# Applying a Fourier layer's score modes: elementwise on three engines instead of two-diagonal matrix products

## The chip, the cores and the metric

One Trainium2 chip, one of its cores. A core has five engines with queues of their own: TensorE (PE in the profile; its weight loads are PEld), VectorE (DVE), ScalarE (ACT), GpSimd (POOL) and SyncE (SP, which here issues most of the DMAs). Each engine works through its queue in order and waits on semaphores for the others. Matrix products read SBUF and write PSUM; DVE and ACT read both memories, and POOL works on SBUF here. All arithmetic is float32. The metric is the device time of one execution in microseconds (us), and lower is better.

## What is computed

Two layers of the same kind, each `x = x + layer(groupnorm(x))`, on `x` of shape (2 images, 56 channels K, 128, 128). Inside a layer stands an attention over the 56 channels whose keys, queries and values are Fourier layers with 8 heads A. Cut to what matters here (the layer's text in the reference is longer; `b` image, `i` input, `o` output):

```python
def spectral_conv(x, w, b):
    xf = jnp.fft.rfft2(x, norm='forward')
    top = jnp.einsum('bihw,iohw->bohw', xf[:, :, :M1, :M2], _c(w[0]))
    bot = jnp.einsum('bihw,iohw->bohw', xf[:, :, -M1:, :M2], _c(w[1]))
    of = jnp.zeros((B, Co, H, W // 2 + 1), dtype=xf.dtype)
    of = of.at[:, :, :M1, :M2].set(top).at[:, :, -M1:, :M2].set(bot)
    y = jnp.fft.irfft2(of, s=(H, W), norm='forward')
    return y + b[None, :, None, None]
...
('K', 1, A), ('Q', 1, A), ('V', 1, A), ('P', A, 1), ('M0', 1, 1), ('M1', 1, 1)
```

With M1 = M2 = 16 only 32 x 16 complex modes of each channel take part. The score of channels k and l in head a is a sum over space of query times key; by Parseval's rule it is a sum over the modes of `conj(X_k) * u_a * X_l`, where the complex number `u_a`, one for each mode and head, is made of the weights of K and Q. What the spectral part doesn't hold comes from the Gram matrix of the channels. This complex number times mode is the work that the change moves.

## The kernel before

**Work and order.** The program is first written as a list of *units* (class `Work`): one call, or several that stay together, each with the engines that may do it: T (PE), V (DVE), S (ACT), G (POOL), Q (the SP queue). `ORDER`, a string, then gives every unit once with the letter of the engine that does it, in the order in which it is issued: each number is the step from the unit named before. A small `v` is DVE too, and makes the next POOL unit wait for the end of that one (`issue`). `PLACES` gives for every PSUM buffer that is taken the bank where it lies. Both strings are the result of a search. `AWAKE` lists 40 products on constants that the order puts between the others; they only keep TensorE's clock up.

**Stages of a layer**, for each image b: the plane is turned and normalised (`turned`, `modes_chain`), and its modes are made. `xf` (128 x 448) holds them: eight blocks t of 56 channels; the 128 partitions are two halves e, each with real parts in the first 32 rows and imaginary parts in the next 32. `gram` and `gram_chain` make the channels' Gram matrix with 256 products; then come `scores`, `values`, `softmax_chain`, `mix_chain`, `heads` and `norms_chain`, then the GELU stage and two more Fourier layers. The two images run interleaved, so that one image's scores stand beside the other's Gram products.

**The numbers.** `prepare` makes each layer's constants. `product` multiplies the weights of K and Q into `u_a`; `place` splits a complex number into parts with masks for the real and imaginary rows, the columns 3 and 4 of the constant `raw`; `relay` turns them by products on TensorE into the layout of the modes, into `tcs` (128 x 8 x 36: 16 columns for the scores, 16 for the values, 4 for the M0 and M1 layers). `build(WUv, tcs, 0)` spreads the 16 score columns into WU, 128 x 4096: for each block t and head a, and in each half, a 64 x 64 matrix whose only non-zero entries lie on two diagonals, real to real and real to imaginary. `build(WTv, tcs, 16)` does the same for the values, in WT.

**`scores`** runs over pairs of blocks t. For each pair, 32 small products (8 heads, 2 blocks, 2 halves; 64 x 64 by 64 x 56) put `u_a * X` into two PSUM banks, one copy by ACT or DVE brings them (128 x 896) into the room `UX`, of which there are two, and `scored` adds `xf` times `UX` to the score bank `sc` with 4 products. After four pairs two more products add the Gram matrix's part, and `softmax_chain` starts on DVE. So that four quadrants of the array can work at once, odd blocks come out with their halves exchanged; for them `modes_chain` keeps `xs`, a copy of the odd blocks with exchanged halves (two copies from PSUM of 64 x 224).

WU's room is used again later: `FB[b]`, 1792 columns for each image, takes the modes of the GELU stage and the rows of `h_chain`.

Of the kernel before, what the change touches and what calls it, by code (L numbers as in the profile page):

```python
# [11 lines left out]
ALU = mybir.AluOpType  # L12
# [9 lines left out]
0V 1Q 1S 1S 1Q 1S 1S 1V 1G 1V 1G 1V 1G 1V 1G 1Q 1S 1Q 1S 1Q 1S 1Q 1S 1Q 1S 37T 10G -12T 56G -77T 31Q 17Q -53T  # L22
72Q -60T -18T 17T 28V 20Q 6Q 3Q -73T 11T 26Q -23T 6T 65V -16Q 69G -136T 17T -11T 4T 1T 80T -17Q -1Q 15T -86T 90S
-20Q 21V -4S 1V -53Q 57T 1S 1V -33Q 34T 1S 1V -98T 99T 1S 1V 1T -87T 22Q 44G 22S 1V 1T 2V -72Q -29T 62Q 40T 2V
74V -181T 106S -40Q -57T -8T -6T -4T 191T 1V -80S -26G 370Q -392Q 386Q 7Q -264G 2v 3G -4V -193T 49Q 88T 1S -83Q
145T 1V -142Q 139V -145Q 146V -4T 8T 270Q -269V -134Q 132T 4T -159Q 158T 4T -13S 11V -73T 74T -152Q 1Q 164T -4S
-153Q 146V 1T -157Q 85V 79S 1S -7T 1S 10T 1T 1T 1T 1T -165Q 160S -2S -75G -93Q 92G 2G 1G 1G 1G 1V 1v 77T -76T 7G
57S -136Q -12Q 161T 1T 2S -72V 1V 1V 7T -15V 77V -162Q 66S 21V 7V -10V 11v -33T 102T -168Q 63T 106S -63V 77G
-187Q -11Q 120V -41S -81Q 107V 2T 293Q -392Q 64T 50V 63V -62V 63G -104S 26V -33T 112v -104V -7S 1V -11T -28V 48V
38T 2T 1V -60S 98V -97V 61V -1V -48V 84V 24T -115S 42G 86T -85G 88T -2S 219Q -304G -116Q 188S -64S 10G -66T 1S  # L30
1V 151T -148V 195V -64S -87G 12V 73T 4T 1S 15S -17T 4T 60T -134G 135V 1G -141T 142V 3v 119Q -184S 193Q -195T 9T
-6T 1T 207Q -196G 53S -57T 55S -143S 142v -49V 56T 117Q -404Q 39Q 101G 82T 68T -63V 61V -4G 5T -57S 1V 1T 59T
-2V 1T 4T -91V 89V 1T 10T 1T 1T 1T -112V 113T -103v 91V 1T -63S 1T -13S 79S -205G 42G 81T 1S 78V 11T -273Q 200V
3T 92G 70Q -159T 1T -19S 20T 1T 65T -25V -188V 187G 514v -498V -158G 104S 156Q -162V 71T -60T -10T 72S 19T -287V
757V 1V -607V 3V 113V 2T 490V -451T 452V 5v -480G 3S -86v 69V -14T -54T 67S -63V 1T 101S 457G -561S 53S 44T 1S
-31G 1S -64V -156G 157G 96T 1S -83G -10V 1T 1V -5V 73G -67G 73T 1S -17T 15T 3T -74V 1v 1T 34G -102G 141T 1S -90V
18V 53V -54v 75T 1S -70T 1V -36T 103T 3T 1T 11V -32G -180v 95S 118V 1S -87T 1V -70G 157v -13T 1S 3T -92T 1S 150Q
4T 1V 38Q -3Q -21Q -77S 99Q -90T 47T 1V -47S 8T 64Q 18Q -250G -2G 233Q -70T 1V 52T 15T -60T 1T 1T 435G -538V
151S 1S -218v 610G -382V -108G 50S 62Q -1Q 2T 1V -69T -2T 1V 49S 1S 21T 5S 1S 12Q 1Q -83v 65S 1S 18Q -5T 2Q -1V
5T 1V -135G 50T -328V 329V 85T -82V 95Q -97S 9V -8T 2T 1V 15V 76Q -150G 153Q -53T 58Q 146Q -239T 1V -6G 7G -6V  # L40
7V 86T 5Q -8Q 4V 2Q -88v 71S 1S 351G -332T -4Q 5V 141Q 3Q -26Q 2Q -180S -439T 482S 1S -103T 1S 27T 2V -1v 25T 1S
65T 5S 1S -5S -86T 1V 24T 21T 75G 89Q -163S -51v -68G 159S 118Q -207T 1V -14T 221T -220S 223Q 2Q 190G -193Q -5Q
4V 26Q -2Q -189T 1S 169T 1V 13Q -200V 22T 1V 16T 1S 148T 5S 1S 14Q 175G -340T 1V 145S 201G -6G 7G -188T 1V -159T
1V 177Q -17Q 22Q -3Q -16T 1V 38Q -58S 55Q -183T 1V 3T 1S 144T 5S 1S -149T 317G 7T -323V 326V -165Q -329G 495V
-3V 1V -165Q -38T 1S 39Q -7Q 2T -4Q 5V 26Q -41S -142T 8V 135S -142T 181Q -179S 159T 1V -161S 2T 2S -173G 292T 1S
38T -157V 3V 117T -115V -7S 4T 2T 2T 156S -41V -114V 2V 132T 17S 14T 2Q -11S 14Q -18S 11Q -343G 351T -36S -5T
-129G 2V 159Q 4V -162G 1V 1T 125S 5T 21T 1S 14V 1T 1S -166V 129V -130v 7T 1V 163S 1S -705T 538T 1V 300T 1S 1G 4T
4V -3V 1V 1V -313T 7T -6S -533T 540V 1G 8V 149S -121T 1V 98T 171T -170S 5T -132G 2Q -6T 302S -261V 1G 95V -125T
10V -9V -12S 1S 155T 1S -108T 103T 1S -94V -9V -4T -14G 126T 1V -99G 4Q 104V -8T 1T -114S 1S 114S -154T 155S
-150V 3Q 20Q 26Q -53S 1S -503V 795T -138T -142v 145V -130T -580T 709S 4V 2V -134S -20T 1S 150T 2T -132S 134T -8V  # L50
9V 2V -125G 2Q 122G 2V -112T 113G -112S -59Q 178G 118V -283S 47S -608T 845V -277T 1S -576T 1139Q -412V 1T 2V
-126T 1S -28S 29S 123V 7T 1V -728T 722T 1S 122V 9v -129T 1V -741T 587Q -10Q 293T -862T 863V 1G 6G -19V -856T
555Q 315V 3S 1S -133T 131S -873T 752V -753T 754G -204Q 194V 1G 381Q -364T 1V -186Q 195V 28T 10V 1G -53Q 102T 1S
# [23 lines left out]
2T 3V 2T 1T 29V 47Q -14Q 1Q -67S 5T 1V 1G 57Q 11Q -67V 1V 28Q -5Q -33S 43T 1V 4Q -37G 74T -24Q -49v 1T 3T 1S 92S  # L77
-46Q 21S -9Q 5Q -20Q -11V 3Q -22Q 90S -84Q 85G -76Q 73S 1G -73Q 40T -39Q -33V 93S -92v 4T 1V 17Q -16T 89G -12S
1G -49Q 58G -55Q -2Q 36T -52Q -13V 100T 4V 2S -32S 1G 30Q -4V 1Q -36T 1T 4V 2S 30S -31Q 17T 4V -25S 2S -1Q 9T 4V
8V 2S -13V 5S -4Q 11Q -10S 2Q 12S -1Q  # L80
"""

PLACES = [int(c) for c in (
# [1189 lines left out]
```

## Time and profile before

| | us |
|---|---|
| runs shown | 404.88, 405.82, 1596.27 |
| median of the runs | 405.82 |
| the profiled execution | 403.93 |
| its span in the trace | 402.1 |

One of the three runs, 1596.27, stands far from the others. The profile is of one execution; its mean granted clock is 0.958 of TensorE's full speed. Its page has the busy time of each engine, the span in 40 slices, the chain of work that ended last, and the costliest groups of instructions. Every record here has line 225, that of `issue`, as its source, so groups are told apart by the names of the tiles: `psum<-xf,WU` are the products with the two-diagonal matrices, `P<-psum 128x896` copies of a pair (and of turned planes), `WU<-tc,C` the builds. A product in float32 is recorded as two. In the rows by stretch the columns are: stretch, its length, the busy time of PE, PEld, DVE, ACT and POOL with the number of instructions, the granted clock, the share of the DMA engines, GB/s.

### The profile page before, as it was taken

To read this page: it belongs to the slowest core of one execution; us is meant where nothing else is said; L and a number is where in the kernel's file an instruction comes from. 1 tells how busy PE (TensorE), PEld (TensorE's weight loads), DVE (VectorE), ACT (ScalarE), POOL (GpSimd) and SP (SyncE) were. 2 spreads that over 40 slices of the span, in tenths; PEclk is the share of its full clock that TensorE was granted. 3 is DMA by queue.
4 is the path that set the end of the run, shared out by engine and by line. 5 is a ranking of instruction groups with operands and counts; after the bars stand their busy time and mean duration, and the time that the engine had idled before them with its cause. 6 is when DMAs were issued, how large, how long until landed. Compare 5 with 4: busy or idle time off the path is not lost.

```text
span 402.1 us, 16509 instructions
## 1 busy us (share of the span) xinstructions
PE 364.4 (91%) x7316; PEld 258.3 (64%) x7316; DVE 310.5 (77%) x576; ACT 229.9 (57%) x335; POOL 198.7 (49%) x199
## 2 busy tenths in 40 slices
PE   8879999999989999898899999999999799889960
PEld 5545985897665556567676885797675555557440
DVE  7886798586867987899878858496969966997861
ACT  1425675236448768556958767134469637994520
POOL 9638293426775393158319261122422670268390
PEclk9999999999998999899969999999999789999895
DMA  7878305000044334000401363520053413212766
GB/s 211 216 213 201 79 3 163 3 3 4 20 146 115 93 109 125 13 3 26 136 5 36 110 200 103 173 64 4 13 156 101 139 53 112 91 35 85 223 188 209
DMA packets 21324, 40.04 MB, mean 100 GB/s; under 512 B 4613, under 2 KB 5381, under 8 KB 21253
## 3 DMA queue, kind: packets, MB, share of 16 engines
q1 hardware_dynamic: 20002, 35.25, 30.2%
q10 hardware_dynamic: 1250, 3.74, 3.1%
q8 instruction: 57, 0.93, 1.0%
q14 instruction: 15, 0.11, 0.1%
HBM read 24.29 MB, written 14.68 MB: 97 GB/s over the span
## 4 chain that ended last, share of the span: by engine, by line
PE 56%; DVE 21%; ACT 8%; issue 5%; POOL 4%; DMA 3%; SPq 1%; POOLq 1%; DVEq 0%; ACTq 0%
PE psum L225 56%; DVE X L225 6%; DVE P L225 6%; ACT P L225 5%; POOL P L225 3%; DMA xr<-x 3%; DVE WU L225 2%; DVE stats L225 2%; ACT psum L225 2%; DVE WT L225 1%; SPq L225 1%; ACT WT L225 1%; DVE f L225 1%; POOLq L1267 1%; POOL rs L225 1%
## 5 line engine op out<-in xcount | busy, mean ns | idle before, releaser
L225 ACT COPY P<-psum 128x896 f32<-128x896 f32 (+5 forms) x56 | 45.4, 835 | 53.8 <-PE psum L225 31.1
L225 POOL TENSOR_TENSOR X<-X,gvr 128x1024 f32<-128x1024 f32 x22 | 51.7, 2363 | 22.6 <-DVE P L225 8.2
L225 PE MATMUL psum<-P 128*64 128x56 f32 (+2 forms) x1632 | 59.3, 228 | 0.0
L225 PEld LDWEIGHTS psum<-C,P 32*128 32x128 f32 (+4 forms) x1124 | 44.3, 169 | 22.0 <-issue 6.5
L225 PEld LDWEIGHTS psum<-P 128*64 128x64 f32 (+1 forms) x1632 | 53.1, 138 | 6.7 <-issue 3.4
L225 PE MATMUL psum<-C,P 32*128 32x128 f32 (+4 forms) x1124 | 53.3, 264 | 3.0 <-DVE X L225 1.3
L225 DVE SCALAR_TENSOR_TENSOR X<-psum,cols,xr 128x1024 f32<-128x1024 f32 x32 | 40.3, 1275 | 12.7 <-PE psum L225 7.5
L225 ACT ACTIVATE P<-psum,cols 128x1024 f32<-128x1024 f32 x32 | 35.1, 1110 | 13.0 <-PE psum L225 12.2
L225 POOL TENSOR_TENSOR P<-P,X 128x1024 f32<-128x1024 f32 x13 | 30.4, 2361 | 15.4 <-ACT P L225 12.3
L225 ACT COPY WT<-psum 128x896 f32<-128x896 f32 x28 | 25.1, 903 | 19.3 <-PE psum L225 18.2
L225 PE MATMUL psum<-X,BTx 57*64 57x512 f32 x256 | 35.1, 630 | 1.1 <-ACT psum L225 0.7
L225 DVE STREAM_TRANSPOSE P<-psum 128x448 f32<-128x448 f32 (+1 forms) x24 | 29.1, 1226 | 7.2 <-PE psum L225 7.0
L225 POOL TENSOR_TENSOR X<-P,X 128x1024 f32<-128x1024 f32 x11 | 26.8, 2459 | 14.1 <-DVE WT L225 8.2
L225 ACT ACTIVATE psum<-P 128x1024 f32<-128x1024 f32 x32 | 32.9, 1030 | 0.7
L225 PE MATMUL psum<-P,C 128*64 128x112 f32 (+2 forms) x296 | 30.4, 389 | 2.2 <-ACT WT L225 1.0
L225 PE MATMUL psum<-ones 128*128 128x256 f32 (+1 forms) x80 | 30.9, 519 | 1.1 <-DVE ones L225 1.1
L225 ACT ACTIVATE P<-P,sh,gv 128x1792 f32<-128x1792 f32 x12 | 21.9, 1876 | 10.6 <-DVE sh L225 6.8
L225 PEld LDWEIGHTS psum<-C,X 56*128 56x128 f32 x512 | 18.5, 138 | 9.5 <-issue 4.8
L225 PEld LDWEIGHTS psum<-P,C 128*64 128x64 f32 (+2 forms) x296 | 15.1, 142 | 14.3 <-DVE P L225 5.5
L225 PE MATMUL psum<-C,X 56*128 56x56 f32 x512 | 22.1, 227 | 1.7 <-DMA X<-x 1.1
L225 PE MATMUL psum<-C,WT 32*128 32x128 f32 (+1 forms) x544 | 21.0, 279 | 2.8 <-DVE P L225 1.4
L225 PEld LDWEIGHTS psum<-C,WT 32*128 32x128 f32 (+1 forms) x544 | 18.0, 184 | 6.8 <-issue 2.8
(224 smaller groups left out, 693.5 us busy)
## 6 DMA issues: line engine op xcount, KB each, us to landing
xr<-x SPq DMA_DIRECT2D x64, 112.0 KB
store<-X SPq DMA_DIRECT2D x64, 112.0 KB
xr<-store SPq DMA_DIRECT2D x64, 112.0 KB
X<-x SPq DMA_DIRECT2D x34, 112.0 KB
out<-P SPq DMA_DIRECT2D x32, 112.0 KB
out<-P SPq DMA_DIRECT2D x8, 224.0 KB
out<-P ACTq DMA_DIRECT2D x8, 224.0 KB
stage<-weights SPq DMA_DIRECT2D x4, 272.0 KB
```

The lines of the kernel that those rows point to most:

```text
L225: done = getattr(engines[letter.upper()], method)(*args, **kw)
L1267: with tile.TileContext(nc) as tc:
```

## The change

The number times the mode is made elementwise. With `u = p + iq`, the product's real row is `p*re - q*im` and its imaginary row `p*im + q*re`: the mode times one column, plus its partner row (real for imaginary and the reverse) times another, whose sign is put into the constant `raw`. So `place` isn't needed for the scores, `WU` is no longer built, and odd and even blocks have one form. For each pair of blocks, ACT multiplies `xf` by the first column, head by head and block by block: 16 instructions of 128 x 56 in one unit, into `UX`. DVE or POOL multiplies the partners `xs` by the second column (one operation of 128 x 896) into `FB[b]`, and DVE or POOL adds the two. `xs` is now the whole of `xf` with exchanged groups of 32 partitions: four copies of 32 x 448 that POOL, ACT or DVE may make, in one buffer that both images use. `relay` puts the score columns into `uc`, one buffer for each layer. WU's room shrinks to what `FB` needs.

`ORDER` and `PLACES` are new throughout: 1,528 units for 1,518, and so are the letters. Of the 32 new products and sums 16 are DVE's and 16 POOL's; of the 16 `xs` copies ACT makes 8, DVE 5 and POOL 3. Of ACT's copies of 896 columns 13 are left of 28, and some other units change engines (four scalings of X go from DVE to POOL, two scalings of planes from ACT to DVE). `AWAKE` is unchanged. Ahead of the last score product of their stage stood 1, 2, 2 and 1 of the four units of value products; now 1, 4, 4 and 3.

```diff
-        [own, mirror, -mirror, count * dc * N * re, count * dc * N * im, dc * re, dc * im], 1
+        [own, mirror, -mirror, count * dc * N, count * dc * N * (im - re), dc * re, dc * im], 1
...
-    WU, WT, WM = hold("WU", [N, 4096]), hold("WT", [N, 4096]), hold("WM", [N, 1024])
-    WUv, WTv = (t.rearrange("p (t a m) -> p t a m", t=8, a=HEADS) for t in (WU, WT))
+    WU, WT, WM = hold("WU", [N, 3584]), hold("WT", [N, 4096]), hold("WM", [N, 1024])
+    WTv = WT.rearrange("p (t a m) -> p t a m", t=8, a=HEADS)
...
+    XS, UX = [hold("xs", [N, 448])] * B, [P[b][:, 5344:7136] for b in range(B)]
...
-            place(t64, cpt[:, o : o + 16].rearrange("p (a c) t -> p a c t", c=2), re, im, k)
+            to = cpt[:, o : o + 16].rearrange("p (a c) t -> p a c t", c=2)
+            if k == 3:
+
+                for c, t in enumerate((re, im)):
+                    tt(who, to[:, :, c], t, _bc(rawc[:, k + c], 1, 8), ALU.mult)
+            else:
+                place(t64, to, re, im, k)
...
-        tcs = hold("tc", [N, 8, 36])
+        tcs, uc = hold("tc", [N, 8, 20]), hold(f"uc{layer}", [N, 8, 16])
...
-        build(WUv, tcs, 0)
-        relay(cpt, tcs, stage[:, :1024], 16, 16)
-        relay(cpt, tcs, stage[:, :1024], 32, 4)
-        build(WTv, tcs, 16)
+        relay(cpt, tcs[:, :, :16], stage[:, :1024], 16, 16)
+        relay(cpt, tcs[:, :, 16:], stage[:, :1024], 32, 4)
+        build(WTv, tcs, 0)
...
-        xs = P[b][:, 7840:8072]
-        clear("GV", xs[:, 224:], 0.0)
-        for e in range(2):
-            q, o = slice(64 * e, 64 * e + 64), slice(64 - 64 * e, 128 - 64 * e)
-            copy(
-                "SV", xs[o, :224].rearrange("p (u k) -> p u k", k=K),
-                px[q, :448].rearrange("p (u v k) -> p u v k", v=2, k=K)[:, :, 1, :],
-            )
+
+        xs = XS[b]
+        for q in range(0, N, 32):
+            copy("GSV", xs[q : q + 32], xf[q ^ 32 : (q ^ 32) + 32, :448])
...
-        def scored(t):
-            u = R["UX"][t // 2 % 2]
+        uc, xs = prs[L][2].rearrange("p t (a c) -> p c t a", c=2), grid(st["xs"])
+        for t in range(0, 8, 2):
+            flat = [r[:, 896 * (t // 2 % 2) : 896 * (t // 2 % 2) + 896] for r in (UX[b], FB[b])]
+            both = [z.rearrange("p (t a k) -> p t a k", t=2, a=HEADS) for z in flat]
+            with work.unit():
+                for k in range(2):
+                    for a in range(HEADS):
+                        S.activation(both[0][:, k, a], xv[:, t + k], AF.Copy, scale=uc[:, 0, t + k, a : a + 1])
+            tt("GV", both[1], _bc(uc[:, 1, t : t + 2], 3, K), _bc(xs[:, t : t + 2, :], 2, HEADS), ALU.mult)
+            tt("GV", flat[0], *flat, ALU.add)
             with work.unit():
                 for k in range(2):
                     score(
-                        (xf[:, K * t : K * t + 64], st["xs"][:, K * t // 2 : K * t // 2 + 64])[k],
-                        grid(u[:, 448 * k : 448 * k + 448]), start=(t + k == 0), stop=False,
+                        xf[:, K * t + K * k : K * t + K * k + 64], grid(flat[0][:, 448 * k : 448 * k + 448]),
+                        start=(t + k == 0), stop=False,
                     )
-
-        for t in range(0, 8, 2):
-            p = pair()
-            with work.unit():
-                for a in range(HEADS):
-                    for k in range(2):
-                        for e in range(2):
-                            o = e ^ k
-                            T.matmul(
-                                p[64 * o : 64 * o + 64, k, K * a : K * a + K], lhsT=WUv[64 * e : 64 * e + 64, t + k, a, :],
-                                rhs=xv[64 * e : 64 * e + 64, t + k, :], start=True, stop=True,
-                                tile_position=(64 * e, 64 * o), skip_group_check=True,
-                            )
-            copy("SV", R["UX"][t // 2 % 2].rearrange("p (k m) -> p k m", k=2), p[:, :, :448])
-            scored(t)
```

More of the change, by code (lines that the diff above doesn't have):

```diff
@@ L27 @@
[L27 to L41, printed above, removed]
```

129 lines of the change are left out of this document (72 added, 57 removed).

## The prediction

> **What bounds the kernel now.** I read the page first: busy times, then the chain that ended last.
>
> ```profile
> span 402.1 us, 16509 instructions
> PE 364.4 (91%) x7316; PEld 258.3 (64%) x7316; DVE 310.5 (77%) x576; ACT 229.9 (57%) x335; POOL 198.7 (49%) x199
> PE 56%; DVE 21%; ACT 8%; issue 5%; POOL 4%; DMA 3%; SPq 1%; POOLq 1%; DVEq 0%; ACTq 0%
> ```
>
> TensorE (PE) is busy for 91% of the span and carries 56% of the chain; ScalarE (ACT) is busy for 57%. That is an average. The change works in four stages, one for each layer and image: from the copy that makes the modes `xf` to the first softmax operation, which reads the finished scores. The timeline gives their ends; here are the start of the first stage and the ends of the first and the last.
>
> ```profile
> 40.48 0.51 ACT L225 COPY xf<-psum 128x448 f32<-128x448 f32 x1
> 65.00 0.40 DVE L225 TENSOR_TENSOR psum<-psum,rr 128x224 f32<-128x224 f32 x1 [0.47 <-PE psum L225]
> 282.31 0.38 DVE L225 TENSOR_TENSOR psum<-psum,rr 128x224 f32<-128x224 f32 x1
> ```
>
> The view of busy time by stretches, asked for these four, and then for the tile WU alone over stretches that hold the products which leave (last row):
>
> ```profile
> 40.50:65.00 24.50, 24.44 (x699) 20.72 (x699) 19.86 (x61) 16.65 (x23) 14.27 (x13) 1.00 0.24 57
> 78.30:103.30 25.00, 24.86 (x675) 20.86 (x674) 19.57 (x57) 10.55 (x16) 11.66 (x19) 1.00 0.02 4
> 225.50:247.70 22.20, 21.91 (x623) 18.09 (x622) 14.67 (x29) 16.51 (x29) 11.09 (x8) 1.00 0.47 144
> 263.20:282.30 19.10, 18.88 (x560) 15.87 (x561) 15.26 (x42) 6.00 (x11) 4.67 (x6) 1.00 0.05 14
> sum 90.80, PE 90.10 PEld 75.53 DVE 69.36 ACT 49.71 POOL 41.68; mean PE 22.52 PEld 18.88 DVE 17.34 ACT 12.43 POOL 10.42
> sum 71.00, PE 18.27 PEld 16.59 DVE 1.22 ACT 0.00 POOL 8.80; mean PE 4.57 PEld 4.15 DVE 0.30 ACT 0.00 POOL 2.20
> ```
>
> The columns are stretch, length, PE, weight loads, DVE, ACT, POOL, then the granted clock. In the four stages PE is busy for 90.10 of 90.80 us, so they are PE's: what leaves PE there can shorten them, until another engine fills them. The reader should keep two sums: PE has 18.27 us to give, and ACT has 90.80 - 49.71 = 41.1 us of room.
>
> **What is removed.** These groups hold the durations:
>
> ```profile
> L225 PE MATMUL psum<-xf,WU 64*64 64x56 f32 x1024 | 18.3, 220 | 0.0
> L225 ACT COPY P<-psum 128x896 f32<-128x896 f32 x28 | 24.6, 908 | 30.9 <-DMA X<-x 11.0 <-PE psum L225 10.7 <-DVE stats L225 6.0
> L225 ACT COPY P<-psum 64x224 f32<-64x224 f32 x6 | 2.0, 340 | 8.6 <-PE psum L225 8.5
> L225 POOL TENSOR_TENSOR WU<-tc,C 128x1024 f32<-128x1024 f32 x7 | 13.3, 1913 | 11.5 <-ACT tc L225 10.8 <-DVE vd L225 0.7
> L225 DVE TENSOR_TENSOR WU<-tc,C 128x1024 f32<-128x1024 f32 x1 | 1.2, 1216 | 0.0
> L225 DVE COPY P<-psum 128x896 f32<-128x896 f32 x4 | 4.3, 1083 | 3.7 <-PE psum L225 3.7
> L225 POOL TENSOR_TENSOR stage<-stage,C 128x64 f32<-128x64 f32 x8 | 2.4, 321 | 2.3 <-DVE P L225 2.3
> ```
>
> The 512 products with WU go (1024 records, two each): PE -18.3 us, 4.6 a stage. Sixteen copies of their results go; by the new order's letters ACT makes 13 copies of 896 columns where it made 28, so ACT -15 x 24.6/28 = -13.2 us, and DVE 3 for 4 (-1.1). ACT loses 6 half copies, -2.0. The eight builds of WU go: POOL -13.3, DVE -1.2. In `product` six small operations become two in each layer; they lie ahead of the first stage on engines that are not full, and I put them at nothing (8 x 0.32 us, the last row's, would be gained if the first stage waited for them).
>
> **What is added on ACT.** 64 multiplications of 128x56 a stage, each with a scale read from a column of numbers, 256 in all. The nearest row is a 56x56 one of the same kind; its start to the next start tells what it takes of the queue:
>
> ```profile
> 238.15 0.33 ACT L225 ACTIVATE vd<-C,vc 56x56 f32<-56x56 f32 x1
> 238.38 0.90 ACT L225 ACTIVATE P<-psum 128x896 f32<-128x896 f32 x1
> ...
> 54.34 0.21 ACT L225 COPY rr<-psum 128x57 f32<-128x57 f32 x1
> 54.44 0.29 ACT L225 COPY tc<-psum 128x128 f32<-128x128 f32 x1
> ...
> L225 ACT COPY xf<-psum 128x448 f32<-128x448 f32 x3 | 1.6, 524 | 0.0
> L225 ACT ACTIVATE P<-P,sh,gv 128x1792 f32<-128x1792 f32 x12 | 21.9, 1876 | 10.6 <-DVE sh L225 6.8 <-PE psum L225 3.9
> L225 ACT COPY P<-psum 128x1024 f32<-128x1024 f32 x14 | 13.9, 1010 | 6.0 <-PE psum L225 3.5 <-DMA out<-P 2.4
> ```
>
> It lasts 0.33 us and the next begins 0.23 after it. I take 0.23: 256 x 0.23 = 58.9 us. The bounds: with no overlap 0.33 (84 us); and 0.10 (26 us), the step of the copy `rr`, which has the width but reads PSUM and has no column for a scale. The first row has both the source and the scale of the new operation, so I stay with it. The partner copies `xs` are new: four of 32x448 a stage, 16 in all, of which the order gives ACT 8, DVE 5, POOL 3. They replace the half copies; between 0.34 (64x224) and 0.53 (128x448) I take 0.5: ACT +4.0. The new order also hands DVE two plane scalings (ACT -2 x 1.88) and two copies of 1024 (-2.0). ACT net: 58.9 - 13.2 - 2.0 + 4.0 - 3.8 - 2.0 = +41.9 us, nearly all inside the stages: 49.7 + 41.9 = 91.6 us of work in stages that last 90.8. **So ACT takes PE's place as the bound**, and PE, at 90.1 - 18.3 = 71.8, waits for it.
>
> **What is added on DVE and POOL.** 32 products and sums of 128x896, by the letters 16 on each.
>
> ```profile
> L225 POOL TENSOR_TENSOR P<-P,X 128x1024 f32<-128x1024 f32 x13 | 30.4, 2361 | 15.4 <-ACT P L225 12.3 <-DVE P L225 3.1
> L225 DVE TENSOR_TENSOR X<-X,gvr 128x1024 f32<-128x1024 f32 x10 | 11.9, 1212 | 0.0
> L225 DVE TENSOR_SCALAR P<-P,gv,sh 128x1792 f32<-128x1792 f32 x4 | 4.7, 1207 | 0.1
> L225 DVE COPY P<-psum 128x1024 f32<-128x1024 f32 x4 | 4.9, 1222 | 5.5 <-PE psum L225 5.5
> ```
>
> 896/1024 of these: DVE 1.06 us each, 17 in all; POOL 1.67 (the kind with a spread operand, as WU's build) to 2.07, together 30. With the moved work (two scalings of 1.21, two copies of 1.22, five `xs` of 0.5; four scalings of X by 1.21 and one WU build fewer, one copy of 1.1 less) DVE is at 69.4 + 17 + 2.4 + 2.4 + 2.5 - 4.8 - 1.2 - 1.1 = 86.6 of 90.8: almost full as well. POOL: 41.7 + 30 - 13.3 + four scalings of X (9.4) + 1.5 = 69, the smaller shifts left out.
>
> **How long the stages become.** An engine with 91.6 us of work is not packed without gaps. ACT's densest slices of ten us:
>
> ```profile
> 190.00:200.00 10.00, 8.30 (x149) 6.45 (x145) 8.85 (x27) 9.79 (x22) 3.69 (x4) 1.00 0.42 128
> 340.00:350.00 10.00, 9.18 (x120) 5.38 (x114) 8.81 (x25) 9.58 (x14) 1.09 (x3) 1.00 0.41 124
> 350.00:360.00 10.00, 7.68 (x133) 4.27 (x134) 10.00 (x10) 9.17 (x13) 6.86 (x3) 1.00 0.03 8
> ```
>
> Their mean is 95%: 91.6/0.95 = 96.4, so the stages grow by 5.6 us. UX is a ring of two: from the third pair on, the 16 multiplications wait until the scores of the pair before last have read their buffer, and behind them on ACT stand the plane scalings of the other image, copies of value products and the exponential of the softmax; that wait is in the 5%. `xs` is one buffer for both images: image 1's copies wait for image 0's last product, a whole stage earlier, at no cost.
>
> Credit: while PE waits for ACT it can do what it now does after the stage.
>
> ```profile
> L225 PE MATMUL psum<-WT,xf 64*64 64x256 f32 x256 | 17.1, 384 | 0.0
> ```
>
> These are 16 units of 17.1/16 = 1.07 us. In the order of before 6 of them stand ahead of the last score product of their stage, in the new one 12: 6 x 1.07 = 6.4 us of PE's later work are moved under ACT.
>
> **The sum.** Profiled execution 403.93 us (span 402.1 and 1.8 around it). 403.93 + 5.6 - 6.4 = 403.1. Two of the runs shown, 404.88 and 405.82, stand 1.4 above the profiled one on the mean: **404 us**, against a median of 405.82. A difference under 2%, 8 us, is about what a measurement of this kernel can tell from no change.
>
> **Rivals.**
>
> *Faster: PE stays the bound.* If the small multiplications pack nearer to 0.10 us (at 0.10 ACT needs 58 us, not 91.6), or the new order runs ACT far ahead of PE, the stages give back what the chain had in them. The shares of the chain by engine, asked for 40 to 70 us and for 225 to 290:
>
> ```profile
> by line: PE psum L225 80.3%; ACT P L225 15.2%; POOL gv L225 2.0%; DVE var L225 1.5%; issue 0.9%; DVE sh L225 0.7%; DVE gs L225 0.6%; ACT tc L225 0.2%; DVE nm L225 0.2%; ACTq L225 0.1%
> by line: PE psum L225 76.3%; DVE P L225 7.1%; issue 6.9%; POOL rs L225 2.2%; ACT psum L225 1.7%; ACT P L225 1.6%; POOL vc L225 0.9%; DVE top L225 0.6%; DVE psum L225 0.6%; DVE vd L225 0.6%; DVE vc L225 0.6%; ACT vd L225 0.4%; DVE sqk L225 0
> ```
>
> 78% of 18.3 is 14.3 us: 403.9 - 14.3 + 1.4 = 391 us. For it: PE's share there. Against it: the 91.6 us of ACT. Chance 0.25.
>
> *Slower: DVE and POOL block each other.* Products and sums of two SBUF tensors do not seem to run on both at once:
>
> ```profile
> 227.35 2.34 DVE L225 TENSOR_TENSOR WT<-tc,C 128x1024 f32<-128x1024 f32 x2
> 228.64 3.28 POOL L225 TENSOR_TENSOR X<-P,X 128x1024 f32<-128x1024 f32 x1 [8.21 <-DVE WT L225]
> ```
>
> POOL's sum lasted 3.28 us instead of 2.36, as if it had stood until DVE's second product ended at 229.69: 0.92 lost. With 32 more of them, and DVE at 86.6 of 90.8 us, such waits fall on the way to the scores. At 0.92 for half of the 32, 15 us: on top of the growth of 5.6 and less the credit this is 403.1 + 15 + 1.4 = 419; it decides once DVE's work and its waits pass ACT's 96, that is from some ten collisions on. Against it: the order keeps a POOL operation behind a DVE one by its letter `v`. Chance 0.22.
> The Trainium skill, in "SBUF — State Buffer", section "SBUF: two separate sides", has it as a rule: the two engines share one pair of ports, whoever starts first holds it for the whole instruction and the other stands. By that rule, the trace agrees (0.92 us).
>
> *PE's clock drops while it waits.*
>
> ```profile
> 200.00:210.00 10.00, 9.73 (x64) 6.85 (x64) 7.04 (x18) 4.99 (x9) 0.86 (x2) 0.66 0.08 25
> ```
>
> In this slice the granted clock is 0.66: 3.4 us of full clock lost. If PE's waits for ACT brought one such slice in two of the four stages, and PE had become late by it: 403.1 + 6.8 + 1.4 = 411. Against it: PE at 71.8 of 96 us has room for that. Chance 0.05, half of it past 2%.
> The Trainium skill, "TensorE: Matmul & The Clock Gate", Part 1, says that an idle window of about 3.4 us halves the clock; by it a PE that waits for ACT longer than that pays. No stage of before shows it: their clock is 1.00.
>
> **The numbers.** My forecast has 0.48, all within 2% (397.7 to 413.9). Faster by over 2%: 0.25. Slower: 0.22 + 0.03 = 0.25. Within: 0.50. The range, 391 to 417, reaches to the faster rival's time and most of the way to the slower one's, and leaves out the farther part of each, some 2 in 10; the bound of 0.33 us for a multiplication (25 us more on ACT, spread over stages that could not hide it) is left out with the slower one's.
>
> **What would show it.** In the profile after: PE about 346 us busy, ACT about 272, DVE about 328, POOL about 220. The 256 multiplications should show starts 0.23 apart; the four stages should sum to some 96 us with ACT at 95% and PE under 85%; value products should stand inside them. Were PE still at 99% there, the faster rival is right; were POOL sums of over 2.07 us or DVE products of over 1.06 frequent and ACT not full, the slower one. I am wrong in the premise if the stages move where the order lets other work fill them, so that their length tells nothing of the end.

## The result, and the profile after

| | before | after |
|---|---|---|
| median of 20 runs, us | 404.0 | 407.8 |
| lowest, highest, us | 400.79, 1596.27 | 405.36, 414.0 |
| the profiled execution, us | 403.93 | 408.25 |
| its span; mean granted clock | 402.1; 0.958 | 406.5; 0.949 |

The ratio of after to before is 1.010, with a 95% interval of 1.0068 to 1.0133. A ratio leaves out the slower executions of each kernel and a median takes in all, so a ratio can differ from that of two medians. The change costs one per cent; I had forecast half a per cent the other way.

The page of the kernel after, its span, its busy times, and TensorE's granted clock in 40 slices:

```profile
span 406.5 us, 14733 instructions
PE 354.2 (87%) x6292; PEld 242.8 (60%) x6292; DVE 328.0 (81%) x607; ACT 271.1 (67%) x565; POOL 219.7 (54%) x198
PEclk9988998999999999799959998999999999999995
```

PE lost 10.2 us of busy time and its idle time grew from 37.7 to 52.3 us (span less busy). ACT, DVE and POOL have gained what the operations cost. The new operations, by the views of the tiles `uc` and `WU` (count: shortest/median/longest in ns, first and last start), the last two being the sums:

```profile
L225 ACT ACTIVATE P<-xf,uc x256: 324/330/356, 48.2 to 290.8; 128x56 f32<-128x56 f32 x128
L225 DVE TENSOR_TENSOR WU<-uc,xs x8: 1076/1088/1093, 48.7 to 273.9; 128x896 f32<-128x896 f32 x8
L225 POOL TENSOR_TENSOR WU<-uc,xs x8: 1697/1702/1705, 49.9 to 283.2; 128x896 f32<-128x896 f32 x8
L225 POOL TENSOR_TENSOR P<-P,WU x8: 2073/2093/2099, 53.1 to 291.3; 128x896 f32<-128x896 f32 x8
L225 DVE TENSOR_TENSOR P<-P,WU x8: 1075/1084/1093, 66.1 to 287.4; 128x896 f32<-128x896 f32 x8
```

Each price is within 3% of the one that the prediction took. The four stages, by the view of stretches:

```profile
42.93:70.70 27.77, 26.11 (x437) 19.07 (x435) 23.59 (x52) 24.75 (x78) 17.79 (x18) 0.94 0.30 65
78.55:109.50 30.95, 30.36 (x659) 23.97 (x655) 26.15 (x66) 25.57 (x84) 12.65 (x15) 1.00 0.11 31
231.46:260.60 29.14, 25.49 (x459) 18.05 (x455) 22.17 (x39) 26.82 (x87) 10.73 (x9) 0.94 0.60 181
266.11:295.00 28.89, 27.33 (x563) 21.61 (x563) 21.10 (x47) 23.62 (x80) 15.03 (x15) 1.00 0.02 4
sum 116.75, PE 109.28 PEld 82.70 DVE 93.01 ACT 100.76 POOL 56.19; mean PE 27.32 PEld 20.68 DVE 23.25 ACT 25.19 POOL 14.05
```

They grew by 26 us, not by 5.6, and PE is full in them all the same (109.3 of 116.8 us, 94%), although 18 us of its products are gone. So the stage is no longer the right stretch to compare: other work has been put into it. Longer stretches have the same work in both kernels: up to the first `xf`; from there to the first copy of `h_chain` in layer 0; on to layer 1's first `xf`; from there to the first copy of `h_chain` in layer 1; the end. Before:

```profile
0.00:40.50 40.50, 35.38 (x383) 22.18 (x384) 30.71 (x46) 14.78 (x16) 27.60 (x37) 1.00 0.79 210
40.50:155.80 115.30, 111.22 (x2543) 81.22 (x2543) 89.02 (x198) 68.18 (x97) 68.18 (x94) 0.99 0.25 70
155.80:225.50 69.70, 64.37 (x1176) 46.65 (x1178) 60.44 (x104) 47.78 (x80) 28.87 (x19) 0.93 0.16 47
225.50:332.50 107.00, 102.41 (x2376) 75.39 (x2371) 79.65 (x148) 60.46 (x92) 41.31 (x32) 0.97 0.34 101
332.50:402.10 69.60, 51.06 (x859) 32.88 (x858) 50.70 (x81) 38.67 (x54) 32.77 (x18) 0.91 0.44 135
```

And after:

```profile
0.00:42.90 42.90, 33.50 (x353) 19.92 (x353) 33.22 (x60) 13.94 (x14) 25.35 (x29) 0.92 0.79 194
42.90:160.10 117.20, 109.78 (x2073) 76.22 (x2073) 99.65 (x203) 88.21 (x214) 66.37 (x81) 0.99 0.26 70
160.10:231.50 71.40, 63.20 (x1116) 44.29 (x1118) 60.80 (x108) 47.34 (x78) 40.16 (x33) 0.88 0.13 39
231.50:338.30 106.80, 97.70 (x1906) 69.14 (x1902) 80.90 (x154) 82.11 (x209) 56.98 (x39) 0.98 0.36 107
338.30:406.40 68.10, 50.00 (x860) 33.19 (x860) 53.42 (x84) 39.49 (x54) 30.87 (x19) 0.92 0.45 135
```

The second and the fourth stretch hold the scores: 115.3 to 117.2 and 107.0 to 106.8 us, together +1.7. In the fourth PE has 4.7 us less to do and waits 4.5 us longer. In the second its work fell by only 1.4 us; the view of the tile `ones`, the AWAKE products, from image 0's variance to the first copy of `h_chain`, tells why (the first number behind the length is PE). Before, and then after:

```profile
28.50:155.80 127.30, 3.37 (x12) 1.47 (x10) 0.00 (x0) 0.00 (x0) 0.99 0.30 82
```

```profile
29.10:160.10 131.00, 12.67 (x36) 5.90 (x35) 0.00 (x0) 0.00 (x0) 0.97 0.33 82
```

The new order has moved 9.3 us of them there, 7.5 of these into the second stretch itself (2.65 us before, 10.16 after). Of the other stretches the first is 2.4 us longer, the third 1.7, the last 1.5 shorter. All these rows are of one execution each, and the first and the third don't hold steady. In the kernel after PE waited 5.9 us in the first for the DMA of the constants, in the one before not at all. In the runs below that keep the units of these two stretches the first `xf` came at 40.4 to 43.3 us, and the third took 68.8 to 71.7.

### The profile page after: what moved, and what is told of

The parts are those of the page before. It is cut to its first block, busy times and chain, and to the rows that moved or that the text cites. A ratio compares the mean times of both kernels' runs of the same rounds, so it can differ in the third digit from the quotient of the medians.

```text
span 406.5 us, 14733 instructions
## 1 busy us (share of the span) xinstructions
PE 354.2 (87%) x6292; PEld 242.8 (60%) x6292; DVE 328.0 (81%) x607; ACT 271.1 (67%) x565; POOL 219.7 (54%) x198
## 5 line engine op out<-in xcount | busy, mean ns | idle before, releaser
L225 POOL TENSOR_TENSOR X<-X,gvr 128x1024 f32<-128x1024 f32 x26 | 61.3, 2371 | 21.8 <-DVE P L225 10.4
L225 ACT ACTIVATE P<-xf,uc 128x56 f32<-128x56 f32 x256 | 60.8, 334 | 1.8 <-PE psum L225 1.7
L225 PEld LDWEIGHTS psum<-C,P 32*128 32x128 f32 (+4 forms) x1124 | 42.6, 162 | 24.0 <-issue 7.7
L225 PE MATMUL psum<-C,P 32*128 32x128 f32 (+4 forms) x1124 | 51.2, 255 | 5.2 <-DVE P L225 1.8
L225 PE MATMUL psum<-P 128*64 128x56 f32 (+1 forms) x1568 | 50.3, 223 | 0.5 <-ACT P L225 0.5
L225 PEld LDWEIGHTS psum<-P 128*64 128x64 f32 (+1 forms) x1568 | 48.1, 138 | 4.2 <-ACT P L225 1.5
L225 ACT COPY P<-psum 128x896 f32<-128x896 f32 (+4 forms) x34 | 28.9, 878 | 29.4 <-PE psum L225 13.8
L225 POOL TENSOR_TENSOR P<-P,X 128x1024 f32<-128x1024 f32 x11 | 25.9, 2365 | 21.1 <-ACT P L225 8.0
L225 PE MATMUL psum<-P,C 128*64 128x112 f32 (+2 forms) x296 | 29.0, 381 | 1.6 <-ACT psum L225 0.8
L225 PEld LDWEIGHTS psum<-ones 128*128 128x128 f32 x80 | 15.9, 223 | 12.9 <-issue 6.8
```

What stands on the lines that cost most here:

```text
L225: done = getattr(engines[letter.upper()], method)(*args, **kw)
```

## The experiments

Ratios are to the kernel before, with 95% intervals; where nothing else is said, a kernel is that of after with the edit shown.

### The form in the old order, and less work for ScalarE or for DVE and POOL

`old_order` gives `ORDER` and `PLACES` of before to the new form; the units that replace one another stand at the same places (an `xs` copy that would come ahead of `xf` stands right behind it).

> The elementwise form in the order of before: each unit of 16 multiplications stands where the products with WU stood, its partner product right behind it, the sum where the copy stood, the xs copies at the half copies; the banks of before. Everything else is as in the kernel after. Theory A (ScalarE's multiplications, in series and behind the Gram products, lengthen the way to the softmax): slower than before, 410 to 420 us, and the stages above 90.8 us in sum. Theory B (the new order costs the time, above all its front with the half clock at 27 us, and not the form): 404 us or less, as before. Theory C (DVE and POOL in each other's way): slower too, but with DVE products over 1.1 us or POOL sums over 1.7.

`short_l0` and `short_l1`, and later `short_both`:

```diff
-                    for a in range(HEADS):
+                    for a in range(1 if L in (0,) else HEADS):
                         S.activation(both[0][:, k, a], xv[:, t + k], AF.Copy, scale=uc[:, 0, t + k, a : a + 1])
```

> The kernel after with 2 multiplications a pair of blocks instead of 16 in layer 0 alone: the first product is made for head 0 only and left out for the other seven. ScalarE's unit falls from 3.83 us to some 0.6. Theory A: the two stages of layer 0 (27.8 and 31.0 us) shrink to 22 to 25 each and the first GELU product, 5.3 us late against before, comes 4 to 6 us earlier; time 402 to 404. Theory B: stages shorten, the time stays 407 to 408. Theory C: no change, since the partner products and sums are all there: 407 to 408 with stages as long as now.

> The same in layer 1 alone. Theory A: stages of 29.1 and 28.9 us shrink to some 22 each; since other work of PE was put into them, the end follows by less than that, 1 to 5 us: 403 to 407. If the time that layer 1's stages grew by is all refilled: 408, no change. Theories B and C: no change, 408.

`no_partner`:

```diff
-            tt("GV", both[1], _bc(uc[:, 1, t : t + 2], 3, K), _bc(xs[:, t : t + 2, :], 2, HEADS), ALU.mult)
-            tt("GV", flat[0], *flat, ALU.add)
```

> The kernel after without the partner products and the sums, in both layers: the score products read what ScalarE made, and 16 operations of DVE and 16 of POOL are gone (the imaginary-to-real part is left out). Theory C (DVE and POOL are the way): back to 403 us or less. Theory A: the part of the chain that is one partner sum per pair goes, 1.1 to 1.7 us for each of the last pairs of the stages, and the rest stays: 405 to 407. Theory B: 408.

| | median us | ratio | interval |
|---|---|---|---|
| old_order | 472.8 | 1.175 | 1.162 to 1.188 |
| short_l0 | 406.0 | 1.007 | 1.002 to 1.012 |
| short_l1 | 406.6 | 1.010 | 1.005 to 1.016 |
| no_partner | 405.0 | 1.007 | 1.002 to 1.012 |

In the old order the form costs 69 us. Its stages, in an execution of 481.5 us, by the view of stretches (the third, and the sum of the four):

```profile
262.40:307.60 45.20, 28.01 (x379) 19.13 (x379) 17.02 (x31) 30.83 (x90) 17.26 (x12) 0.62 0.42 131
sum 161.80, PE 105.66 PEld 74.53 DVE 94.19 ACT 104.01 POOL 70.13; mean PE 26.41 PEld 18.63 DVE 23.55 ACT 26.00 POOL 17.53
```

PE idles for 56 of 161.8 us and its clock falls. Nobody is full: as I read it, the multiplications stand in ScalarE's queue at places chosen for products of PE, and each waits there or makes others wait. So the new order isn't what costs time (Theory B); it earns back nearly all of what the form costs in an unfitting one.

But neither does ScalarE's work by itself set the time (Theory A). The first two stages of `short_l0`:

```profile
41.60:68.40 26.80, 24.89 (x437) 18.79 (x437) 23.74 (x53) 12.54 (x22) 16.66 (x16) 1.00 0.36 78
76.20:106.10 29.90, 29.90 (x659) 23.93 (x655) 25.95 (x66) 13.55 (x28) 12.42 (x13) 1.00 0.10 32
```

ScalarE (the fourth engine of the row) is down from 50.3 to 26.1 us in these two stages, and they are 2 us shorter. In `short_l1` the third stage is 1.2 us shorter (27.9), and the time is as it was (1.010). Why no more, is to be seen in `short_l1` at the end of that stage, in the timeline of DVE and of PE (start, length, instruction, in brackets the wait and who ended it):

```profile
249.46 2.33 DVE L225 TENSOR_SCALAR P<-P,gv,sh 128x1792 f32<-128x1792 f32 x2
251.71 2.08 DVE L225 TENSOR_TENSOR P<-P,WU 128x896 f32<-128x896 f32 x2
```

```profile
252.85 1.98 PE L225 MATMUL psum<-P,xf 128*64 128x224 f32 x16 [1.03 <-DVE P L225]
```

ScalarE's last multiplication there ended at 249.4. The two sums stand on DVE behind two plane scalings of the other image, in the order that suited the long multiplications, and PE waits for them. In the kernel after the same score product waits for the multiplication instead, which ends at 255.7; the sum follows at once.

### The AWAKE products

Theory A2 was formed here: in stage 00 PE waits for other engines and the AWAKE products only fill the wait. Theory D: they take time from PE. `drop_awake` leaves out the 10 AWAKE units between 54 and 98 us; `drop_awake_short` has in addition the edit of `short_l0`; `awake_front` moves 9 of them behind the last AWAKE unit ahead of the first mean product, into its bank.

> The kernel after without the 10 AWAKE products that its order puts between 54 and 98 us (8.3 us of PE; 9 of them in stage 00). They compute nothing that is used. Theory D (the new order spends layer 0's saved products on AWAKE products in a stretch where PE is full): the first GELU product comes 5 to 8 us earlier, 400 to 403 us. Theory A2 (PE waits there for ScalarE's multiplications and the AWAKE products only fill the wait): PE's idle time in stage 00 rises by about 8 us, the stage stays within 2 us of 27.8, and the time within 2 us of 407.8, or above if the clock falls.

> The same without the 10 AWAKE products, and with 2 multiplications a pair instead of 16 in layer 0 (the first product made for head 0 only there). Theory A2: now both the wait and its filling are gone, stage 00 falls to 18 to 22 us and the time to 400 to 402. Theory D: like the run without the AWAKE products alone, the shorter multiplications add nothing.

> The kernel after with 9 of these 10 AWAKE products moved ahead of the first mean product of the front, into the 5.9 us in which PE waits there (from 22.4 to 28.3 us). Theory E (the half clock of 6.8 us at 27 us delays layer 0): the half clock at 27 us is gone, xf of image 0 comes 2.5 us earlier, as before, and with Theory D's gain the time is 398 to 402. Theory A2: xf comes earlier by 2.5 us, and the time falls by that, to 405; stage 00 stays.

They took 408.1 us (1.014, 1.003 to 1.025), 405.9 (1.008, 1.003 to 1.012) and 408.2 (1.012, 1.004 to 1.020). Stage 00 of `drop_awake`, and of `drop_awake_short`:

```profile
43.30:70.80 27.50, 24.42 (x417) 17.94 (x417) 23.62 (x53) 24.71 (x78) 17.50 (x18) 0.81 0.28 58
```

```profile
42.30:69.70 27.40, 21.91 (x419) 16.43 (x419) 23.60 (x53) 12.53 (x22) 18.04 (x18) 0.89 0.28 67
```

Without the AWAKE products the stage is as long as in the kernel after, 27.5 for 27.8 us. By the view of the tile `ones` 5.9 us of them are gone there, yet PE is busy for only 1.7 us less: the granted clock falls from 0.94 to 0.81, and the other products take longer. So leaving them out gains nothing and Theory D is out; whether PE waits for others there, or the lower clock takes back what was freed, this run doesn't tell. A2 is out in its second half: without the multiplications too the stage stays at 27.4, at a clock of 0.89. In `awake_front` the first `xf` did come earlier, at 42.4 for 42.9 us, not by the 2.5 expected, and the time didn't follow.

### What PE's products were worth

`before_one_head` is the kernel before with one edit, and `before_twice` with its opposite:

```diff
-                for a in range(HEADS):
+                for a in range(1):
                     for k in range(2):
...
                             T.matmul(
                                 p[64 * o : 64 * o + 64, k, K * a : K * a + K], lhsT=WUv[64 * e : 64 * e + 64, t + k, a, :],
```

```diff
-                for a in range(HEADS):
+                for a in [*range(HEADS)] * 2:
```

> The kernel before, its own order, with the products with WU made for head 0 only: 4 of 32 in each unit; the copies and all else stay, the other seven heads' numbers are left out. It asks what the 18.3 us of PE were worth where they stood. Theory F (they are worth their PE time, and the elementwise form takes the gain back): 16 x 28/32 of 1.14 us, 16 us off: 386 to 392 us. Theory G (other waits stand right behind them, so PE idles instead): 398 to 403 us, PE idle time up by over 10.

> The kernel before with every product with WU made twice into the same place: 512 more small products a layer, 18.3 us of PE more. All is computed. Theory J (balanced order: PE and the chains of the other engines each hold the stages, so less on PE gives nothing and more on PE costs nearly all of it): 415 to 421 us. Theory K (PE's products in the stages are hidden behind other waits in both directions): 404 to 408.

With an eighth of the products the kernel before took 401.6 us, ratio 0.997 (0.984 to 1.009). The two stretches that hold the scores, and then its first two stages and the sum of the four:

```profile
40.50:154.50 114.00, 106.72 (x2095) 74.71 (x2095) 90.52 (x199) 67.43 (x97) 68.21 (x94) 0.97 0.25 70
223.80:329.00 105.20, 95.26 (x1926) 67.79 (x1922) 79.42 (x148) 60.35 (x91) 41.31 (x32) 0.98 0.34 103
```

```profile
40.50:66.50 26.00, 24.45 (x477) 18.60 (x477) 19.90 (x61) 17.47 (x24) 14.32 (x13) 0.87 0.26 63
79.60:104.40 24.80, 22.44 (x456) 18.04 (x453) 20.07 (x58) 10.16 (x17) 11.67 (x19) 1.00 0.01 2
sum 91.90, PE 82.95 PEld 64.41 DVE 69.75 ACT 49.84 POOL 43.03; mean PE 20.74 PEld 16.10 DVE 17.44 ACT 12.46 POOL 10.76
```

PE has 11.7 us less to do in the two stretches, and they are 3.1 us shorter; the stages are as long as they were, 91.9 for 90.8. PE waits there for ACT's and DVE's results, by a microsecond at a time; over the whole span its idle time grows by 8.6 us, where Theory G had asked for over 10. Waits are not all of it. In the first stage the granted clock is 0.87 where the kernel before had 1.00, and PE is busy as long (24.45 for 24.44 us) with fewer products; in the fourth it is 0.91. In the second and the third, at 1.00, PE has 2.4 and 3.3 us less to do, and the stages are only 0.2 and 1.0 us shorter.

Made twice, the products cost all of their time: 422.75 to 435.46 us in four runs, the shortest 19 above the median of the kernel before measured beside it (403.57). In the profile, of an execution of 433.06 us, the four stages, at a granted clock of 1.00, sum to

```profile
sum 116.20, PE 108.13 PEld 92.00 DVE 69.70 ACT 50.44 POOL 41.88; mean PE 27.03 PEld 23.00 DVE 17.42 ACT 12.61 POOL 10.47
```

That is 25.4 us more for 18.0 of PE; how much of the excess belongs to this one execution is open. So Theories G and J: more on PE costs in full, less gives little, by the interval at most 1.6% where 16 us are 4%. PE is the bound only by a hair; behind it stand the other engines' results and, in two stages, the clock. That the search for an order is what brought the queues so close to one another is my reading, and no run tests it.
The Trainium skill, "Perfetto Trace Analysis", section "Identifying the Most-Contended Engine", says that the busy share of matmuls misleads about TensorE's headroom, that the share of peak arithmetic (MFU) and the share of weight loads are the better signs, and that the engine with the highest occupancy comes first. Over the whole span before, the weight loads have 64% against DVE's 77%, and by this PE was the wrong engine to relieve. But over the four stages, where the products stood, they have 83% (75.53 of 90.80 us) against DVE's 76%, and there the rule names PE too. So it foretells neither that less on PE gave 0.3% nor that doubling costs in full.

### What the form costs in its own order

`free_awake` joins `short_both` and `no_partner`: nearly nothing of the form is left. `free_all` leaves out the 10 AWAKE units as well.

> The kernel after, its own order, with the elementwise form made nearly free: 2 multiplications a pair instead of 16 (head 0 only) in both layers, no partner products and no sums; the AWAKE products stay. Theory F: all that the form costs is gone and PE is 18 us shorter than before: 386 to 394 us. Theory G (no engine's share of the form sets the time, the order's other chains do): 400 to 405.

> The same, and without the 10 AWAKE products between 54 and 98 us. Theory D: another 5 to 8 us less than the run that keeps them. Theory G: within 2 us of it, the clock lower in stage 00.

> The kernel after with 2 multiplications a pair instead of 16 in both layers (the first product made for head 0 only). Theory H (ScalarE's multiplications carry the cost of the form): near the run in which the whole form is nearly free, 397 to 400 us. Theory I (two chains in parallel, ScalarE's multiplication and the sums behind other work in the queues of DVE and POOL, each long enough to hold the score alone): 404 to 407.

| | median us | ratio | interval |
|---|---|---|---|
| after | 407.8 | 1.010 | 1.007 to 1.013 |
| short_both | 406.8 | 1.006 | 0.997 to 1.014 |
| no_partner | 405.0 | 1.007 | 1.002 to 1.012 |
| free_awake | 396.9 | 0.994 | 0.988 to 1.000 |
| free_all | 398.3 | 0.994 | 0.988 to 0.999 |

The form costs 1.6% in its own order (1.010 less 0.994), some 6 us. ScalarE's part alone gives back 0.4, DVE's and POOL's alone 0.3, both together all of it; the first two lie within the uncertainty. The stretches that hold the scores show where, in one execution each. Layer 0's in `short_both`, in `no_partner` and in `free_awake`:

```profile
41.70:156.10 114.40, 108.33 (x2071) 76.51 (x2068) 99.55 (x203) 63.85 (x102) 66.52 (x81) 1.00 0.27 72
41.30:157.50 116.20, 108.95 (x2071) 75.99 (x2071) 92.98 (x196) 88.14 (x214) 49.41 (x72) 1.00 0.25 69
40.40:155.10 114.70, 107.91 (x2072) 75.79 (x2071) 92.83 (x196) 63.94 (x103) 49.20 (x72) 1.00 0.29 75
```

The kernel after has 117.2 there. Here ScalarE's multiplications by themselves are the cost: without them the stretch is as short as without the whole form (114.8 in `short_l0` too), as Theory H has it, and 7 us less on DVE with 17 less on POOL give 1.0. Layer 1 is different; its stretch in `short_both`, in `no_partner` and in `free_awake`:

```profile
225.40:333.30 107.90, 97.25 (x1908) 68.56 (x1902) 82.23 (x154) 57.63 (x97) 57.02 (x39) 0.98 0.35 106
```

```profile
226.30:334.10 107.80, 101.05 (x1910) 69.39 (x1906) 71.90 (x144) 82.09 (x210) 46.22 (x32) 0.97 0.35 106
```

```profile
223.90:325.40 101.50, 95.80 (x1908) 68.24 (x1904) 71.06 (x145) 57.58 (x98) 46.23 (x32) 1.00 0.38 113
```

After has 106.8. Taking 25 us from ScalarE gives nothing, taking 9 from DVE and 11 from POOL gives nothing, taking both gives 5.3 us. In layer 1 this is Theory I: two chains lead to a score product, the multiplications and the sums behind other work, and either is long enough. How far single executions differ, `awake_front` above and `awake_gap` below show, which keep the whole form: 116.0 and 116.4 us in layer 0, 109.7 and 108.4 in layer 1. So the 2.5 us of layer 0 and the 5.3 of layer 1 are clear of that, the 1.0 is not.

And the other side: with the form nearly free and 18 us of products gone, the kernel would be 0.6% faster than before (0.0 to 1.2; by the medians, 396.9 us for the 403.2 of the kernel before measured beside it, 1.6). That is about all that there was to win, and 391 us, my faster rival, was not to be had in either order.

### Other ways to make the numbers

`two_products` leaves the sum to the score bank, which adds up its products anyway; `two_drop` leaves out the 10 AWAKE units too; `two_pool` gives the third pair's first product to POOL.

```diff
-            tt("GV", flat[0], *flat, ALU.add)
             with work.unit():
-                for k in range(2):
-                    score(
-                        xf[:, K * t + K * k : K * t + K * k + 64], grid(flat[0][:, 448 * k : 448 * k + 448]),
-                        start=(t + k == 0), stop=False,
-                    )
+                for z in flat[::-1]:
+                    for k in range(2):
+                        score(
+                            xf[:, K * t + K * k : K * t + K * k + 64], grid(z[:, 448 * k : 448 * k + 448]),
+                            start=(t + k == 0 and z is flat[1]), stop=False,
+                        )
```

> The kernel after without the 16 sums: the score bank, which adds up anyway, takes 8 products a pair instead of 4, with the partner products and with ScalarE's. All is computed. DVE loses some 9 us, POOL some 17, PE gains 16 x 1.0 = 16. Theory I: the chain of each pair is 1.1 to 2.1 us shorter: 401 to 405. If PE's time is what counts: 412 to 420. Theory H: 407 to 409, the sums don't matter.

> The same without the 10 AWAKE products between 54 and 98 us. If PE has become the bound of stage 00 by the added products, 3 to 6 us less than the run with them; if the chain of ScalarE is, no change.

> As two_products, and the first product of the third pair of each stage is one operation of 128 x 896 on POOL (1.7 us) instead of 16 multiplications on ScalarE. ScalarE loses 15 us, POOL gains 7. Theory H: 2 to 4 us less than two_products. Theory I: within 2 us of it, or more if POOL's queue has other work in front.

Against what is written there, not all is computed as it should be: in this order of the eight pairs whose buffer of partner products is used again, five are overwritten by the later pair before the score products have read them. The number, place and engine of the operations are as described. They took 411.1 us (1.025, 1.015 to 1.035), 411.7 (1.027, 1.018 to 1.036) and 415.1 (1.034, 1.020 to 1.049). The stages of `two_products`:

```profile
sum 121.80, PE 118.12 PEld 91.17 DVE 87.51 ACT 101.69 POOL 41.14; mean PE 29.53 PEld 22.79 DVE 21.88 ACT 25.42 POOL 10.29
```

PE has 8.8 us more there and the stages are 5 us longer, with PE at 97%: again, what is added to PE costs. The sums are gone and nothing is gained by it: Theory I had put this run at 401 to 405 us, and the chain that became shorter gave less than the products on PE cost. `two_drop` came out like `two_products`, so the added products aren't what holds stage 00, or the clock takes back there what the AWAKE products leave; the runs don't separate the two. Taking work from ScalarE and giving POOL half of that (`two_pool`) didn't help either; its interval overlaps the others.

`pool_product_drop` makes the first product of all pairs one operation on POOL:

```diff
-            with work.unit():
-                for k in range(2):
-                    for a in range(HEADS):
-                        S.activation(both[0][:, k, a], xv[:, t + k], AF.Copy, scale=uc[:, 0, t + k, a : a + 1])
+            tt("GV", both[0], _bc(uc[:, 0, t : t + 2], 3, K), _bc(xv[:, t : t + 2, :], 2, HEADS), ALU.mult)
```

> The first product too as one operation of 128 x 896 a pair, on POOL (1.7 us by the rows of the kernel after), in place of the 16 multiplications of ScalarE (3.83 us), in both layers, and without the same 10 AWAKE products; all is computed. ScalarE loses 61 us, POOL gains 27. Theory A2: the chain of a pair shortens by some 2 us, the time is 400 to 404. Theory C (DVE and POOL in each other's way): POOL products above 2.1 us, the time above the run that only drops the AWAKE products. Theory D: as that run.

It took 438.0 us (1.086, 1.077 to 1.096): against the kernel after ScalarE is busy for 58 us less, and POOL's 30 more, as I read the trace, stand in series with its other products and sums of the same pair. Half of Theory C is seen here, by the view of the tile `uc`:

```profile
L222 POOL TENSOR_TENSOR P<-uc,xf x16: 1692/1698/2709, 48.8 to 313.5; 128x896 f32<-128x896 f32 x16
L222 DVE TENSOR_TENSOR WU<-uc,xs x8: 1076/1091/2585, 48.6 to 296.6; 128x896 f32<-128x896 f32 x8
```

The longest of each is 1.0 and 1.5 us above its median; in the kernel after the longest product or sum is within 9 ns of the median on both engines. So they can hold each other up with these very operations, and in the kernel after the order kept them apart.

### The clock at the change of layers

`awake_gap` moves 9 of the AWAKE units of 54 to 98 us to 186 to 212 us, into free banks.

> The kernel after with 9 of the 10 AWAKE products of 54 to 98 us moved to the change of layers (some 186 to 212 us, where the order of before has five). Theory E (the half clock there costs about 1 us of PE's way to layer 1's variance): the half clock at 201 us shortens from 10.2 to 3.4 us or goes, the way from image 1's last modes of layer 0 to layer 1's first variance falls from 17.8 to 16.7 us, and the time to 405 to 407. Without Theory E: 407 to 409.

It took 407.8 us (1.015, 1.006 to 1.024). The way from image 1's last `h_chain` copies to layer 1's first variance, after and in `awake_gap`:

```profile
195.70:213.50 17.80, 13.91 (x171) 11.38 (x171) 14.72 (x40) 12.23 (x26) 7.45 (x5) 0.71 0.14 41
```

```profile
190.00:208.00 18.00, 15.24 (x187) 11.21 (x187) 14.99 (x40) 12.64 (x27) 7.76 (x6) 1.00 0.13 41
```

The clock went from 0.71 to 1.00 and the way stayed as long. Theory E is out: PE isn't what this stretch waits for. The longer half clock of the kernel after is no cost here. In the profiled execution of this run the first `xf` came at 40.4 us, as early as before; it took 404.4 us, the shortest of four with a median like that of after. So what part of the 1% the first stretch has, stays open.

## Why the prediction was wrong

The range held the time (391 to 417) and the outcome lay within 2%, as my likeliest case said, but I forecast 404 (the sum, 403.1 and 1.4, is rather 404.5) against a median of 405.8, slightly faster, and it became 1% slower.

**Prices: right.** A multiplication takes 0.33 us and the next begins 0.23 after it (16 in 3.83 us). ACT 271.1 us busy for the 272 forecast, DVE 328.0 for 328, POOL 219.7 for 220 (though the terms written out for POOL come to 226, and the shifts that make up the rest are not named). PE is at 354.2, not 346: its products at the scores are the forecast 18.3 us fewer, and the others took 8 us more, some of it at the lower granted clock.

**"91.6/0.95 = 96.4, so the stages grow by 5.6 us": wrong.** This is the step that failed, with its partner, "6 x 1.07 = 6.4 us of PE's later work are moved under ACT". The stages grew by 26 us to 116.8, with ACT at 86% and PE at 94% where I had put under 85%. With other work moved into them their length tells nothing, as the last sentence of the prediction allowed. Taken over the two stretches that hold the scores, my 5.6 - 6.4 = -0.8 us was +1.7, and +2.5 and +3.4 in the executions of `awake_gap` and `awake_front`, which keep the whole form. For the rest of the program the sum had no term; it took 2.6 us more in the profile after and 2.0 less in that of `awake_gap`, so single executions don't settle it.

**What stood behind that step** was that PE's freed time would be room in which its later work is done for nothing. The runs show that it was worth next to nothing: 16 x 28/32 of a unit's 1.14 us gone, and the time within its uncertainty (0.997, 0.984 to 1.009). That PE is busy for 90.10 of 90.80 us didn't make the stages PE's. On the other side the form costs 1.6% in its own order, some 6 us: in layer 0 by ScalarE, as I had it, in layer 1 by two chains in parallel, where I had one engine at 95%. An order that is 0.6% better with the form nearly free, and 1.6% for the form, make the 1%.

**The rivals.** *Faster*: its sign nearly came, PE at 94% in the stages, but by work that was moved there, and its price was wrong: 78% of the chain there was PE's, but with the products gone others end last. *Slower* by the lock: the products and sums keep to 9 ns of their median in the kernel after, so not there; it caught two `xs` copies (below), whose product then ended at 237.4, while its sum waited for ScalarE until 242.5. *The clock*: lower, 0.94 in two stages; at the change of layers it cost nothing, and in the stages no run measures its price by itself.

What stays open is which of the other chains is next in the order of before: PE's waits there were spread over ACT's copies, DVE's and the Gram matrix's small steps, and no run took one of them away alone. Nor did a run hold the clock up in `before_one_head`, to tell what its fall to 0.87 and 0.91 took back.

## What to carry to other kernels

A stage in which one engine is 99% busy need not be bound by it alone: where other engines' results come just behind, taking work from it gives little and adding costs in full. So measure what removal is worth before building the replacement: leave most of the work out, run it, and see what the best case is (here 0.3 and 0.6%, by the intervals at most 1.6). Look at the granted clock in that run too: it can fall and hide a part of the gain. And where work can move across a stage's borders, compare stretches that hold the same work in both kernels.

## What the runs showed of the hardware

I had put every `xs` copy of 32x448 at 0.5 us. By the view of the tile it took 0.57 us on ACT, 0.39 on DVE, and on POOL 0.56 once and 1.54 twice:

```profile
L225 ACT COPY xs<-xf x8: 562/566/568, 43.5 to 268.7; 32x448 f32<-32x448 f32 x8
L225 DVE COPY xs<-xf x5: 381/388/388, 43.8 to 267.8; 32x448 f32<-32x448 f32 x5
L225 POOL COPY xs<-xf x3: 557/1537/1545, 232.5 to 235.7; 32x448 f32<-32x448 f32 x3
```

The timeline of the kernel after has the three in a row on POOL, and beside them on DVE two products of two SBUF tensors:

```profile
232.54 3.75 POOL L225 COPY xs<-xf 32x448 f32<-32x448 f32 x3 [4.07 <-DVE xs L225]
```

```profile
232.44 1.23 DVE L225 TENSOR_TENSOR X<-P,X 128x1024 f32<-128x1024 f32 x1
233.58 0.54 DVE L225 TENSOR_SCALAR nm<-xf 1x56 f32<-1x56 f32 x1
234.05 1.21 DVE L225 TENSOR_TENSOR WT<-tc,C 128x1024 f32<-128x1024 f32 x1
236.33 1.09 DVE L225 TENSOR_TENSOR WU<-uc,xs 128x896 f32<-128x896 f32 x1 [1.08 <-POOL xs L225]
```

The first copy ends at 234.08, 0.41 us after DVE's first product, the second at 235.68, 0.42 after its next; the third, with no such product beside it, takes 0.56. So a POOL copy too stands while DVE works on two SBUF tensors, and DVE's next product then waited 1.08 us for it.
The Trainium skill, "SBUF — State Buffer", section "SBUF: two separate sides", has the ports that the two engines share as an exclusive lock for a whole instruction; the trace agrees.
